# Ordering the graphs' part of a four-layer graph network with the builder's finer engine model

## Chip, core and metric

The kernel runs on one core of a Trainium2 chip. The metric is the device time of one execution in microseconds (us). The engines are TensorE (PE, with its weight loads as PEld), VectorE (DVE), ScalarE (ACT), GpSimd (POOL) and SyncE (SP), which issues the DMAs.

## What is computed

64 graphs of 256 nodes with 128 features pass through four graph layers. Each adds its result to its input and normalizes every node's features:

```
x = layernorm(x + L0(x, adj))   # h[i] = max over j of relu(p[i] + q[j] + b) * adj[i, j]
x = layernorm(x + L1(x, adj))   # elu of three projections, adj @ in, adj^T @ out, tanh(update)
x = layernorm(x + L2(x, adj))   # two GCN steps: norm_A @ (h @ W) + b, elu between
x = layernorm(x + L3(x, adj))   # msg = gelu(layernorm(mj[j] + mi[i] + b1)); agg = sum of msg * adj
...                             # over neighbours; updated = layernorm([x, agg] @ W2 + b2)
```

The adjacency is a matrix of zeros and ones with about 12% ones. L0 and L3 work on every pair of neighbours and make up most of the work.

## The kernel before

Each graph has its 256 nodes in two halves of 128 partitions. The pair layers don't work on all 65,536 pairs: nodes are sorted by their number of neighbours, each node's neighbours are numbered (`rank`), and a table of slots (`RECTS`, 40 slots, 4800 columns per half, `WIDTH`) says how many nodes have at least so many neighbours. A one-hot matrix `hot` (fp8) has one column per pair of slot and node. A matmul with it brings each neighbour's features to that column.

The work of one graph is in four stages, Python generators that `yield` between steps:

- `first` (L502): loads x and adj, transposes adj (matmuls L516, copies `aT` L519), counts and sorts (L528 to L560: VectorE's `kc` L542, ScalarE's four `sign` L551, VectorE's `perm` L560), permutes (L566, L577, copies `nzp` L571, `permT` L581), makes `rank` (L587) and `lack` (L591), writes the table of full slots to memory with eight DMAs (L620), builds `hot` on VectorE in 24 steps (L629, L635), splits the features q into three bf16 parts (`split3`: copy L497, L498 to L500), and takes the maximum over neighbours: per 512 columns three matmuls (L665) and small ones (L681) into a psum piece `bigp`, folded into `lanes` by VectorE (L492; the first piece by ScalarE, L683). It ends with the layernorm.
- `second` (L778, `layer_1` L215): layer 1, with projections (L223, L230), elu (Exp at L194, L200 and L201), aggregation (L238, L240) and update (L249, Tanh L254).
- `third` (L782, `layer_2` L261): the two GCN steps: scaling L293, adjacency matmul L296, copy `agg` L299, weight matmul L304, L308; a double Exp (L194, L198); then the start of layer 3: projections L797, copies L803 and L497, `dT` (L815), and `sums_of` for the first four tiles.
- `last` (L821): the rest of layer 3. It works on ten tiles (five per half: four of 1024 columns and one of 704; tiles 0 to 4 and 5 to 9). `sums_of` (L718) makes a tile's sums with the one-hot matmuls (L728, into `bigp`) and VectorE's additions (L732), squares them (L736), sums the squares (L743, L745) and sends the row to memory (L750). For each pair of tiles it loads the rows back in another layout (`vr`, L762), takes the root and reciprocal (L768: Sqrt L74, reciprocal L75), multiplies by the full slots (L769), and writes the scales to memory (L771). `fetch` (L825) reads them back spread over all partitions (`rs_s`, L828, three buffers). Then a tile is multiplied by its scales (L839), passes Gelu (L841) and is folded into the sums (L492). The end is the aggregation (L860 to L865), the update (L325, L870, L330) and two layernorms, with the output at L336.

`steps` (L881) runs the four stages as a pipeline over the 64 graphs, all unrolled: in step u, `last` works on graph u, `third` on u+1, `second` on u+2, `first` on u+3. `together` (L341) takes the generators' pieces in turn by the share done. This gives the program order, which is only a priority. The builder then orders each engine's instructions itself: it plays the program through a model of the machine, and whenever an engine is free, gives it the ready instruction with the highest priority. Each engine executes the resulting order as it stands. A table load is put before an activation whose function isn't in the table set then loaded; the set of Gelu, that of Exp (with Tanh) and that of Sqrt are needed in turn, while copies, squares and signs stay in the set that is there.

Pools bound how far stages run ahead. `ps_big` (the `bigp` pieces) and `ps_mm` have four psum pieces each, most tiles of `work` and `pair` have one buffer, `hot` has four, `pre` seven.

After the graphs a few instructions test whether a graph broke the table's bounds (`viol`); a general version of the kernel, `general`, is behind a branch and isn't run with these inputs.

Of the kernel before, what the change touches and what calls it, by code (L numbers as in the profile page):

```python
# [43 lines left out]
def kernel(  # L44
# [77 lines left out]
    with tc.tile_pool(name="prep", bufs=1) as prep, tc.tile_pool(  # L122
        name="ps_prep", bufs=2, space=bass.MemoryType.PSUM
# [217 lines left out]
    def together(*gens):  # L341

        gens = [[0, n, gen] for n, gen in gens]
        while gens:
            e = min(gens, key=lambda e: e[0] / e[1])
            e[0] += 1
            if next(e[2], gens) is gens:
                gens.remove(e)
# [5 lines left out]
    def sparse(ctx):  # L354
# [526 lines left out]
        def steps(g0):  # L881
            ss = [{} for _ in range(U)]
            for u in range(1 - len(STAGES), U):
                together(*[
                    (n, part(g0 + u + i, ss[u + i])) for i, (part, n) in enumerate(STAGES) if 0 <= u + i < U
                ])

        if U == B:
            steps(0)
        else:  # L890
            with tc.For_i(0, B, U) as g0:
                steps(g0)
# [201 lines left out]
    with ExitStack() as path:  # L1094
        sparse(path)

    with tc.tile_pool(name="flag", bufs=1) as fp, tc.tile_pool(
        name="ps_flag", bufs=1, space=bass.MemoryType.PSUM
# [44 lines left out]
```

## Time and profile before

| | |
|---|---|
| time, three runs | 5727.94 us median (5721.77 to 5736.96) |
| profiled execution | 5731.62 us, of which the span from first to last instruction 5729.7 us |
| mean granted TensorE clock | 0.862 of full speed |
| busy: DVE, PE, ACT | 4834.4, 4529.9, 4275.2 us |
| ACT table loads on the trace | 1,283 ns each, before L841, L74, L194, L198 and a few others |
| DMA | 365 MB, mean 64 GB/s |
| span per graph in steady state | 87.4 us (174.80 us for two) |

The page gives each engine's busy time and its share of the span, then the chain of work that ended last, followed back from the last instruction, and the groups of instructions by line with their count, busy time, mean duration and the idle time of the engine before them with what ended it. A timeline gives start and duration of each instruction, and in brackets the idle time before it and its releaser. A busy TensorE counts modelled ends of pipelined matmuls. The durations used for the sums are those of this one execution.

### The profile page before, as it was taken

To read this page: it belongs to the slowest core of one execution; us is meant where nothing else is said; L and a number is where in the kernel's file an instruction comes from. 1 tells how busy PE (TensorE), PEld (TensorE's weight loads), DVE (VectorE), ACT (ScalarE), POOL (GpSimd) and SP (SyncE) were. 2 spreads that over 40 slices of the span, in tenths; PEclk is the share of its full clock that TensorE was granted. 3 is DMA by queue.
4 is the path that set the end of the run, shared out by engine and by line. 5 is a ranking of instruction groups with operands and counts; after the bars stand their busy time and mean duration, and the time that the engine had idled before them with its cause. 6 is when DMAs were issued, how large, how long until landed. Compare 5 with 4: busy or idle time off the path is not lost.

```text
span 5729.7 us, 83531 instructions
## 1 busy us (share of the span) xinstructions
PE 4529.9 (79%) x27408; PEld 2508.7 (44%) x27408; DVE 4834.4 (84%) x14654; ACT 4275.2 (75%) x6485; POOL 1.9 (0%) x10
## 2 busy tenths in 40 slices
PE   5878878878778778788788788787887887877875
PEld 2444444444444444444444444444444444444443
DVE  6788888888888888888888888888888888888876
ACT  2577777777777777777777777777777777777785
POOL 0000000000000000000000000000000000000000
PEclk8888889889889889888898898898888887888986
DMA  0122222222212221221221222122212212221222
GB/s 22 44 70 63 62 63 72 62 63 66 69 57 70 65 63 63 72 63 62 63 72 62 63 65 70 59 68 65 63 62 72 64 62 63 69 66 60 68 65 74
DMA packets 292813, 365.15 MB, mean 64 GB/s; under 512 B 151952, under 2 KB 210448, under 8 KB 292368
## 3 DMA queue, kind: packets, MB, share of 16 engines
q1 hardware_dynamic: 292368, 359.73, 20.0%
q8 instruction: 217, 3.56, 0.3%
q14 instruction: 228, 1.87, 0.1%
HBM read 345.07 MB, written 14.53 MB: 63 GB/s over the span
## 4 chain that ended last, share of the span: by engine, by line
PE 52%; DVE 29%; ACT 11%; issue 4%; DMA 3%; SPq 0%; DVEq 0%; POOL 0%; ACTq 0%
PE bigp L665 11%; PE bigp L728 8%; DVE pre L839 6%; PE mm L860 5%; DVE lanes L492 4%; PE mm L743 4%; DVE hot L629 4%; DVE pre L732 4%; DVE sums L492 3%; PE bigp L681 3%; DMA rs_s<-scale_line 2%; PE mm L870 2%; PE mm L296 2%; PE mm L699 2%; PE mm L647 2%
## 5 line engine op out<-in xcount | busy, mean ns | idle before, releaser
L665 PE MATMUL bigp<-hot,q 128*128 128x512 fp8e4 (+1 forms) x3840 | 1052.3, 371 | 66.6 <-DVE lanes L492 52.6
L728 PE MATMUL bigp<-hot,c 128*128 128x512 fp8e4 (+1 forms) x3840 | 928.8, 372 | 140.2 <-DVE pre L732 140.2
L732 DVE TENSOR_TENSOR pre<-bigp,dT 128x512 f32<-128x512 f32 (+6 forms) x1664 | 846.3, 530 | 37.8 <-PE bigp L728 33.5
L492 DVE TENSOR_TENSOR lanes<-bigp,lanes 128x512 f32<-128x512 f32 (+6 forms) x1536 | 772.7, 503 | 94.6 <-PE bigp L681 86.9
L839 DVE TENSOR_TENSOR pre<-pre,rs_s 128x1024 f32<-128x1024 f32 (+1 forms) x640 | 732.9, 1150 | 48.6 <-DMA rs_s<-scale_line 48.0
L736 ACT ACTIVATE sq<-pre 128x1024 f32<-128x1024 f32 (+1 forms) x640 | 638.5, 998 | 169.9 <-DVE pre L732 163.9
L841 ACT ACT_TABLE_LOAD x535 | 686.4, 1283 | 9.5
L492 DVE TENSOR_TENSOR sums<-pre,sums 128x1024 f32<-128x1024 f32 (+6 forms) x1024 | 628.8, 614 | 41.2 <-ACT pre L841 40.7
L745 ACT ACTIVATE row<-mm,eps_t 128x256 f32<-128x256 f32 (+1 forms) x640 | 289.6, 453 | 476.9 <-PE mm L743 476.7
L841 ACT ACTIVATE pre<-pre,be,g 128x1024 f32<-128x1024 f32 (+1 forms) x512 | 594.2, 1172 | 57.8 <-DVE pre L839 53.0
L743 PE MATMUL mm<-sq,ones 128*32 128x256 f32 (+1 forms) x5120 | 482.9, 440 | 135.2 <-ACT sq L736 135.2
L74 ACT ACT_TABLE_LOAD x445 | 570.9, 1283 | 7.5
L728 PEld LDWEIGHTS <-c 128*128 128x128 bf16 x3840 | 331.2, 98 | 550.5 <-issue 136.1
L665 PEld LDWEIGHTS <-q 128*128 128x128 bf16 x3840 | 310.8, 97 | 392.6 <-issue 112.0
L296 PE MATMUL mm<-aT,hs 128*128 128x256 f32 x512 | 232.3, 600 | 316.1 <-DVE hs L293 214.8
L629 DVE TENSOR_SCALAR hot<-rank 128x512 fp8e4<-128x512 bf16 (+5 forms) x1536 | 440.5, 348 | 0.0
L681 PEld LDWEIGHTS <-pick 42*128 42x128 bf16 x2944 | 155.8, 95 | 481.5 <-issue 474.2
L296 PEld LDWEIGHTS mm<-aT,hs 128*128 128x128 f32 x512 | 135.6, 293 | 425.8 <-issue 316.1
L860 PE MATMUL mm<-w3u,sums 128*128 128x128 f32 x2048 | 296.7, 289 | 18.4 <-DVE sums L492 16.1
L194 ACT ACT_TABLE_LOAD x221 | 283.5, 1283 | 3.9
L681 PE MATMUL bigp<-lack,pick 42*128 42x36 bf16 (+16 forms) x2944 | 285.7, 187 | 0.0
L860 PEld LDWEIGHTS mm<-w3u,sums 128*128 128x128 f32 x2048 | 254.5, 195 | 37.3 <-issue 17.6
(226 smaller groups left out, 7132.6 us busy)
## 6 DMA issues: line engine op xcount, KB each, us to landing
rs_s<-scale_line SPq DMA_DIRECT2D x512, 512.0 KB
rs_s<-scale_line SPq DMA_DIRECT2D x128, 352.0 KB
an<-in_adj SPq DMA_DIRECT2D x64, 256.0 KB
x<-in_x SPq DMA_DIRECT2D x64, 128.0 KB
line<-row SPq DMA_DIRECT2D x512, 4.0 KB
out<-o SPq DMA_DIRECT2D x64, 128.0 KB
fu<-fulls SPq DMA_DIRECT2D x192, 4.0 KB
vr<-line SPq DMA_DIRECT2D x192, 8.0 KB
```

Of the source, the lines that this page charges most:

```text
L74: nc.scalar.activation(t, t, AF.Sqrt)
L492: nc.vector.tensor_tensor(lanes[:, :k, :w], src[:, i:i + k], lanes[:, :k, :w], op)
L629: nc.vector.tensor_scalar(hot[:, :, at:at + w], rank[:, :, :w], s0 + i + 1.0 - FAR, None, ALU.is_equal, saturate=False)
L665: nc.tensor.matmul(pt[:, :tl], q3[:, i, h], hot[:, h, t0:t0 + tl], start=i == 0, stop=False)
L681: nc.tensor.matmul(o_, l_, r_, start=False, stop=i == len(todo) - 1)
L728: nc.tensor.matmul(pt[:, :bl], c3[:, k, h], hot[:, h, t0 + b:t0 + b + bl], start=k == 0, stop=k == 2)
L732: nc.vector.tensor_add(block(pre[:, b:], n, w, at), block(pt, n, w, at), widen(dT[:, h, :w], n))
L736: nc.scalar.activation(sq[:, :tl], pre[:, :tl], AF.Square)
L743: nc.tensor.matmul(pr[q * Q:(q + 1) * Q, :tl // 4], ones[:, :Q], v4[:, :, q], start=True, stop=True)
L839: nc.vector.tensor_mul(pre[:, :tl], pre[:, :tl], rs[:, :tl])
L841: nc.scalar.activation(msg[:, :tl], pre[:, :tl], AF.Gelu, bias=be3, scale=g3)
L860: nc.tensor.matmul(pt[:, cols], lanes[:, k, cols], w3u[:, 1], start=k == 0, stop=False)
```

## The change

The call that emits all graphs is put into a named block of its own, and that block is ordered with another machine model of the builder, the one with a finer picture of the engines. The instructions, tiles, pools and program order are the same. Table loads aren't instructions of the kernel; they are put in after the ordering, so their number follows from the order. The block adds a branch on each engine at its start and at its end.

```diff
         if U == B:
-            steps(0)
+            with tc.block(name="graphs", schedule_with_timeline_sim=True):
+                steps(0)
         else:
             with tc.For_i(0, B, U) as g0:
                 steps(g0)
```

In the built programs TensorE, VectorE and ScalarE have the same instructions apart from branches, semaphore waits and table loads. The program before has 1236 table loads in the part that is run, the one after 824, one of them ahead of the block.

## The prediction, made before the changed kernel was run

> **What bounds the kernel now.** I read the page's engine sums first, then the chain that ended last, the costliest groups, and at last a stretch of exactly two graphs (2649.0 to 2823.8 us) engine by engine.
>
> ```profile
> PE 4529.9 (79%) x27408; PEld 2508.7 (44%) x27408; DVE 4834.4 (84%) x14654; ACT 4275.2 (75%) x6485; POOL 1.9 (0%) x10
> PE 52%; DVE 29%; ACT 11%; issue 4%; DMA 3%; SPq 0%; DVEq 0%; POOL 0%; ACTq 0%
> L841 ACT ACT_TABLE_LOAD x535 | 686.4, 1283 | 9.5
> L74 ACT ACT_TABLE_LOAD x445 | 570.9, 1283 | 7.5
> L194 ACT ACT_TABLE_LOAD x221 | 283.5, 1283 | 3.9
> ```
>
> No engine is full. VectorE is nearest, idle (5729.7 - 4834.4)/64 = 14.0 us per graph with the ends of the program. ScalarE spends over 1,500 us on changing tables. The stretch of two graphs, columns as engines with busy us:
>
> ```profile
> 2649.00:2823.80 174.80, 140.39 (x859) 77.58 (x858) 151.88 (x458) 135.85 (x207) 0.00 (x0) 0.89 0.21 67
> ```
>
> A graph takes 87.4 us, and VectorE is idle for (174.8 - 151.88)/2 = 11.5 us of it. Its timeline tells where. I cut the period at the layernorm's last step (L180, end 2652.1) and at the second GCN scaling (L293, end 2680.7). The "head", 28.7 us with 5.7 us idle, builds the one-hot matrix and walks the GCN's short dependent steps. The "rest", 58.4 us with 5.5 us idle, is the dense part. Two waits carry the argument, the first in ScalarE's timeline, the second in VectorE's and SyncE's:
>
> ```profile
> 2667.42 1.28 ACT L198 ACT_TABLE_LOAD   x1
> 2668.72 0.51 ACT L198 ACTIVATE elu_e<-elu_e,minus 128x256 f32<-128x256 f32 x1
> 2669.13 1.04 ACT L736 ACTIVATE sq<-pre 128x1024 f32<-128x1024 f32 x1
> 2670.19 1.28 ACT L841 ACT_TABLE_LOAD   x1
> ```
> ```profile
> 2676.97 0.17 DVE L769 TENSOR_TENSOR vr<-vr,fu 108x16 f32<-108x16 f32 x1
> ...
> 2682.12 0.89 DVE L839 TENSOR_TENSOR pre<-pre,rs_s 128x704 f32<-128x704 f32 x1 [0.53 <-DMA rs_s<-scale_line]
> ```
> ```profile
> 2677.28 0.40 SPq L771 DMA_DIRECT2D scale_line<-vr  x1
> 2677.73 0.36 SPq L764 DMA_DIRECT2D fu<-fulls  x1
> 2678.74 0.35 SPq L828 DMA_DIRECT2D rs_s<-scale_line  x1
> ```
>
> In the head ScalarE is packed and pays a table load before almost every Exp, Gelu or Sqrt. From the last step on a row of scales (L769) to its use (L839) the data goes out to memory and comes back: 0.03 to 0.3 us to the write's issue, 1.46 us to the read's, 3.4 us to the use, 5.0 us in all. For a 1024-wide tile the read takes 3.7 us where L839 waited for it: 5.2 us. Here 4.2 us of VectorE work on average stand between; the wait left is 0.5 us.
>
> **What the Trainium skill says.** "ScalarE: Activation LUTs", What ACT_TABLE_LOAD costs: 1283 ns a load and 1380 ns of drain. The trace agrees on 1283, but the next activation starts 0.01 to 0.02 us after the load's end; I take 1283 alone. "DMA: Bandwidth & Descriptors", Anatomy of one DMA: some 2 us fixed per transfer, mostly the receipt of the last byte. The two transfers here take 1.46 and 3.4 to 3.7 us, near that; the trace's are used. "Perfetto Trace Analysis", Tensor Engine Instruction: ScalarE and VectorE execute strictly in order. The trace agrees: VectorE stands 2.84 us at L226 for a matmul, with independent work behind it. So a misplaced instruction costs its whole wait.
>
> **The change, part by part.** I compared the orders of the two built programs engine by engine, laying the durations of this trace on each queue.
>
> *Removed.* Table loads fall from 1236 to 824: before L841 535 to 313, L74 445 to 378, L194 221 to 129, L198 32 to 1. 412 x 1.283 = 529 us of ScalarE work, 8.3 us per graph. No other work changes: VectorE has 75.1 us per graph both ways, TensorE nearly the same sequence. Loads count only where VectorE or TensorE wait for what lies behind them, so the gain must be followed through the head.
>
> *The head.* From the end of the adjacency's transposed copies (L519): in the new order two Gelus, one load, a row and a square come first (6.0 us), four signs (1.9), load and Exp (1.7); L560's permutations end at 9.4, L197 and the second Exp, now without a load, at 10.4; permT, nzp, permT 1.5, the Exp of io 0.6, rank 0.5: one-hot starts at 13.1 (before: 12.6). L200, L201 and L293 now stand ahead of it, so the first GCN matmul (L296) starts at 13.1 behind L599, not 18.2. One-hot and what lies between take 7.3; L308, load, Exp, L200 and L293 end at 23.5 (before: 27.1). From L180 it is 24.8 instead of 28.7 us. But only 19.6 instead of 22.2 us of VectorE work lie in it; 2.6 us have moved to the rest. Idle in the head: 5.2 instead of 5.7. The visible gain of 3.9 us is 0.5 us net.
>
> *The rest, and a new wait.* The rest has 55.5 instead of 52.8 us of VectorE work. The order puts L839 much closer to L769. VectorE work between them, mean over 48 graphs, before and after: tile 0 7.5 and 4.3 us, tile 2 4.5 and 2.8, tile 4 4.2 and 2.0, tile 8 5.5 and 2.4. The round trip is 5.0 to 5.2. Tile 4: 5.0 - 2.0 = 3.0, less 0.2 for another short wait inside: 2.8 us. Tile 8: 5.2 - 2.4 = 2.8 us, 0.9 of which L498 waits anyway for ScalarE's c. Tile 2's 2.4 us fall into the head, where VectorE would wait for the Gelus: nothing more, and 1 us if that cover goes. Tile 0: covered by the wait for L870. Behind L839 of tile 4 stand the splitting of q (L498 to L500), without which L665 can't go on, so TensorE waits too.
>
> *SyncE's queue.* The fetch of vr for the third group (L762) stands behind the write of the second's scales (L771), and ScalarE's Sqrt, then the copy q, behind it: q is ready at about 31 where tile 4 is released at 33; covered. The eight writes L620 (3.4 us) stand ahead of that L771, whose vr is ready later anyway.
>
> *Other waits of the rest.* Before: 5.5 - 0.5 (tile 4) - 0.6 (L498) = 4.4 us (psum pieces L492 and L732, L330, Sqrt). These depend on how evenly the two big matmul streams are interleaved with their readers; the trace doesn't show the new order. Fewer loads and the stalls above give TensorE and ScalarE time to run ahead: 1.5 us at best. Following the queues piece by piece, with part_max 1.0, L732 2.5, L492 0.4, L330 0.6 and a Gelu behind Sqrt's load 1.3, gives 5.8 at worst. I take 3.0.
>
> *Block.* It adds a branch per engine at each end. The graphs could not start before the preparation's end in the old order either (their first load waits 18.7 us for L440): 0 to 5 us, taken as 0.
>
> *Sum of VectorE's idle time per graph:* 5.2 + 2.8 + 2.8 + 3.0 = 13.8 us against 11.5: +2.3 us, times 64 = +147 us. Profiled execution 5731.6 (span 5729.7), within 0.1% of the median 5727.94: 5728 + 147 = 5875 us.
>
> **Rivals.**
> 1. Faster: ScalarE's loads decide. For it: it is packed in the head, and 11% of the chain is its own. If the head comes out 1.5 us shorter than my sum, tile 8's stall is half hidden (1.5) and the other waits fall to 1.5: 3.7 + 2.8 + 1.5 + 1.5 = 9.5, -2.0 us, 5600 us. It decides where the four terms fall below 11.5. Against it: VectorE, not ScalarE, has least room in the rest, and tile 4's distance is 2.0 us in every one of the 48 graphs.
> 2. No change: the new DMA waits replace the old waits on TensorE one for one (5.2 + 2.8 + 1.9 + 1.6 = 11.5): 5728. That nothing is reordered is excluded; loads and order differ.
> 3. Much slower: other waits at 5.8 us and no cover: 16.6, +5.1 us, 6055 us. For it: strict queues, four psum pieces shared by two streams. Against it: each stall lets the other engines catch up.
>
> **Chances and range.** Forecast 0.54, rival 1 0.21, rival 2 0.10, rival 3 0.15. The measurement can tell about 0.3% (17 us). Faster 0.20, same 0.10, slower 0.70. The range takes most of rivals 1 and 3: 5640 to 6010; the slower cases alone 5760 to 6010.
>
> **What would show it.** Right: table loads near 824 and ScalarE near 3,750 us busy; VectorE still 4,834; idle before L839 on the DMA rs_s from 48 to some 250 to 400 us, tiles 4 and 8 foremost; L296 earlier after L519; q's split late behind tile 4. Wrong: DMA waits under 100 us (then the 5 us round trip is covered by waits I didn't see), or the head shorter by more idle than 0.5 us.

## The result, and the profile after

The changed kernel takes 6335.16 us (median of 4 runs, 6321.98 to 6342.91), the kernel before 5725.73 us beside it: ratio 1.106, 95% interval 1.103 to 1.108, 609 us or 9.5 us per graph slower. The direction was forecast, the size (147 us) was not, and the time lies above the range that was given (5640 to 6010).

The page of the changed kernel: engine sums, the chain that ended last, and five of the costliest groups (count, busy us, mean ns, then the idle time before them and what ended it).

```profile
PE 4742.7 (75%) x27408; PEld 2596.6 (41%) x27408; DVE 4954.8 (78%) x14654; ACT 3794.5 (60%) x6073; POOL 1.9 (0%) x10
DVE 31%; PE 29%; DMA 18%; ACT 17%; issue 4%; SPq 0%; ACTq 0%; POOL 0%; DVEq 0%
L839 DVE TENSOR_TENSOR pre<-pre,rs_s 128x1024 f32<-128x1024 f32 (+1 forms) x640 | 738.2, 1156 | 494.0 <-DMA rs_s<-scale_line 491.8
L841 ACT ACT_TABLE_LOAD x313 | 401.6, 1283 | 5.6
L74 ACT ACT_TABLE_LOAD x378 | 485.0, 1283 | 13.7 <-DMA vr<-line 7.2
```

ScalarE has lost its table loads as forecast (busy 4275 to 3794 us), and the time still rose. In the chain that ended last ScalarE went from 11% to 17% and DMA from 3% to 18%: fewer table loads didn't make a shorter chain. The sum that matters is VectorE's. Its idle time, summed in the trace over the gaps before its instructions, grew from 889 to 1380 us, and its busy time from 4834 to 4955 us: 490 and 120 us, together the whole loss. The list of waits, VectorE's own, of the changed kernel (us in total, times, longest us), and then of the kernel before:

```profile
DVE pre L839 <- DMA rs_s<-scale_line: 491.8, 242, 5.4
DVE vr L75 <- ACT vr L74: 271.2, 178, 5.2
DVE sums L492 <- ACT pre L841: 174.7, 126, 2.3
DVE y L330 <- PE mm L870: 45.2, 58, 9.3
```
```profile
DVE io L226 <- PE mm L223: 179.7, 64, 3.1
DVE rest L498 <- ACT q L497: 93.4, 54, 3.4
...
DVE y L330 <- PE mm L870: 72.1, 64, 4.9
DVE fl L604 <- PE mm L599: 51.0, 64, 2.7
...
DVE pre L839 <- DMA rs_s<-scale_line: 48.0, 57, 4.2
DVE sums L492 <- ACT pre L841: 40.7, 67, 2.3
```

The new order does repair what the old one had: the gap before L226 falls to 15 us, before L498 (on q) to 2.5, before L604 to 5. In their place stand the three longest waits, 938 us together (before: 48 us at L839, 29 at L75 and 41 at L492). The first two are at the end of trips through memory. The timeline of the changed kernel, VectorE and then SyncE's queue, shows one of the 242:

```profile
2928.47 0.17 DVE L769 TENSOR_TENSOR vr<-vr,fu 128x16 f32<-128x16 f32 x1
...
2931.13 0.60 DVE L180 TENSOR_SCALAR x<-y,mv,rs 128x128 f32<-128x128 f32 x2
2934.70 2.46 DVE L839 TENSOR_TENSOR pre<-pre,rs_s 128x1024 f32<-128x1024 f32 x2 [2.97 <-DMA rs_s<-scale_line]
```
```profile
2928.66 0.33 SPq L771 DMA_DIRECT2D scale_line<-vr  x1
...
2930.08 0.84 SPq L828 DMA_DIRECT2D rs_s<-scale_line  x2
```

L769 ends at 2928.64. The write is issued at once, the read at 2930.08, and L839 starts at 2934.70: 6.1 us, of which VectorE has work for three. The second wait has the same shape one trip earlier. ScalarE, then VectorE:

```profile
2905.97 0.47 ACT L745 ACTIVATE row<-mm,eps_t 128x256 f32<-128x256 f32 x1 [3.17 <-PE mm L743]
2908.54 0.37 ACT L865 COPY ak<-mm 128x256 f32<-128x256 f32 x1 [2.10 <-PE mm L862]
2909.69 0.22 ACT L74 ACTIVATE vr<-vr 128x16 f32<-128x16 f32 x1 [0.77 <-DMA vr<-line]
```
```profile
2909.93 0.25 DVE L75 RECIPROCAL vr<-vr 128x16 f32<-128x16 f32 x1 [3.50 <-ACT vr L74]
```

The row of sums is ready at 2906.44, goes out and comes back, and the square root runs at 2909.69. ScalarE stands idle for most of this, so no table load is to blame here; VectorE has already arrived at L75 and waits 3.5 us.

### The profile page after: what moved, and what is told of

It reads as the page before. It is cut to its first block, busy times and chain, and to the rows that moved or that the text cites. A ratio compares the mean times of both kernels' runs of the same rounds, so it can differ in the third digit from the quotient of the medians.

```text
span 6340.9 us, 83074 instructions
## 1 busy us (share of the span) xinstructions
PE 4742.7 (75%) x27408; PEld 2596.6 (41%) x27408; DVE 4954.8 (78%) x14654; ACT 3794.5 (60%) x6073; POOL 1.9 (0%) x10
## 4 chain that ended last, share of the span: by engine, by line
DVE 31%; PE 29%; DMA 18%; ACT 17%; issue 4%; SPq 0%; ACTq 0%; POOL 0%; DVEq 0%
DMA rs_s<-scale_line 11%; PE bigp L665 8%; DVE pre L839 6%; DVE hot L629 6%; PE bigp L728 6%; DMA scale_line<-vr 4%; DVE pre L732 4%; DVE sums L492 3%; PE mm L860 3%; ACT pre L841 3%; PE mm L743 2%; PE mm L810 2%; ACT sign L551 2%; ACT sq L736 2%; DVE lanes L492 2%
## 5 line engine op out<-in xcount | busy, mean ns | idle before, releaser
L665 PE MATMUL bigp<-hot,q 128*128 128x512 fp8e4 (+1 forms) x3840 | 1068.0, 381 | 230.3 <-DVE lanes L492 104.7
L839 DVE TENSOR_TENSOR pre<-pre,rs_s 128x1024 f32<-128x1024 f32 (+1 forms) x640 | 738.2, 1156 | 494.0 <-DMA rs_s<-scale_line 491.8
L732 DVE TENSOR_TENSOR pre<-bigp,dT 128x512 f32<-128x512 f32 (+6 forms) x1664 | 836.1, 531 | 13.1 <-PE bigp L728 10.3
L492 DVE TENSOR_TENSOR lanes<-bigp,lanes 128x512 f32<-128x512 f32 (+6 forms) x1536 | 780.6, 508 | 76.6 <-PE bigp L681 41.9
L492 DVE TENSOR_TENSOR sums<-pre,sums 128x1024 f32<-128x1024 f32 (+6 forms) x1024 | 635.5, 621 | 181.1 <-ACT pre L841 174.7
L207 PE MATMUL mm<-ident,x 128*128 128x128 f32 x512 | 163.5, 419 | 540.6 <-DVE x L180 540.6
L728 PEld LDWEIGHTS <-c 128*128 128x128 bf16 x3840 | 349.5, 100 | 397.1 <-issue 119.0
L296 PE MATMUL mm<-aT,hs 128*128 128x256 f32 x512 | 269.3, 654 | 318.7 <-DVE hs L293 318.7
L743 PE MATMUL mm<-sq,ones 128*32 128x256 f32 (+1 forms) x5120 | 466.5, 437 | 47.0 <-ACT sq L736 46.3
L207 PEld LDWEIGHTS mm<-ident,x 128*128 128x128 f32 x512 | 80.7, 200 | 607.6 <-DVE x L180 572.4
L296 PEld LDWEIGHTS mm<-aT,hs 128*128 128x128 f32 x512 | 148.6, 321 | 423.9 <-issue 342.2
L75 DVE RECIPROCAL vr<-vr 128x16 f32<-128x16 f32 (+1 forms) x320 | 79.1, 247 | 271.5 <-ACT vr L74 271.2
```

The source lines that it names most:

```text
L296: nc.tensor.matmul(pa[:, :N], hs[:, h], aT[:, h], start=h == 0, stop=h == H - 1)
L492: nc.vector.tensor_tensor(lanes[:, :k, :w], src[:, i:i + k], lanes[:, :k, :w], op)
L665: nc.tensor.matmul(pt[:, :tl], q3[:, i, h], hot[:, h, t0:t0 + tl], start=i == 0, stop=False)
L728: nc.tensor.matmul(pt[:, :bl], c3[:, k, h], hot[:, h, t0 + b:t0 + b + bl], start=k == 0, stop=k == 2)
L732: nc.vector.tensor_add(block(pre[:, b:], n, w, at), block(pt, n, w, at), widen(dT[:, h, :w], n))
L743: nc.tensor.matmul(pr[q * Q:(q + 1) * Q, :tl // 4], ones[:, :Q], v4[:, :, q], start=True, stop=True)
```

## The experiments

Three theories went in. A: the new order puts the consumers of two trips through memory (rows to L74 and L75, scales to L839) too close behind their producers. B: it does so everywhere, so that what is taken away at one place comes back at the next. C: ScalarE's order makes its results late; a variant, L, says because of table loads that the order knows nothing of. Line numbers in these kernels are shifted by the lines added above.

**The block alone.**

```diff
-            with tc.block(name="graphs", schedule_with_timeline_sim=True):
+            with tc.block(name="graphs"):
```

> The graphs in a block of their own, ordered with the same model as before. Theory (the finer model's order costs the time): 5726 +- 17 us, as before. Rival (the block's boundary costs): near 6335 us.

5730.82 us, ratio 1.000 (0.999 to 1.001). So the block's boundary costs nothing that can be measured, and the order is all of it.

**One trip cut, the order left free.** L839's scales come from a constant row in memory.

```diff
-                    nc.sync.dma_start(rs[:, :TODO[i][2]], s.pop(("scale", i)).broadcast_to([P, TODO[i][2]]))
+                    nc.sync.dma_start(rs[:, :TODO[i][2]], flat[:, :TODO[i][2]].broadcast_to([P, TODO[i][2]]))
```

> Old model; the spread scales rs_s are read from a constant row in memory instead of the row that L771 has written, so L839 waits for no round trip from L769 (the transfers stay, the scales are all ones). Theory (round trips through memory behind in-order queues): little lost here before, so little gained: L839's 49 us and what follows from it, 5620 to 5720 us.

> The finer model, with the same constant row for the scales. Theory (round trips): the 492 us at L839 go, the waits at L75 for the rows' round trip stay, 5750 to 6000 us, that is at most 300 us over the old model with the same cut. Rival (the interleaving itself: dependent VectorE instructions stand side by side, and Gelu and Sqrt are bunched): 6200 us or more.

With the builder's other model 5688.13 us, ratio 0.993 (0.991 to 0.994), as expected. With the finer one 6508.93 us, ratio 1.136 (1.134 to 1.138): the wait for the scales is gone and the kernel is 174 us slower than with it, in the range of the rival (the interleaving itself). The finer model had made yet another order, with 1379 table loads.

**Both trips cut, the order left free.**

```diff
-            nc.sync.dma_start(vr[:rows], line[:, :n].rearrange("o (p k) -> (o p) k", k=PIECE))
+            nc.sync.dma_start(vr[:rows], flat[:, :n].rearrange("o (p k) -> (o p) k", k=PIECE))
```

> The finer model, with constants read back at both round trips: the rows' (vr, L762) and the scales' (rs_s, L828); all transfers stay, the row sums and scales that were computed are not used. Theory (round trips): no wait on a DMA of this chain is left, and fewer table loads show: 5450 to 5700 us. Rival (the interleaving itself): 6100 us or more.

6345.73 us, ratio 1.107 (1.105 to 1.109). Theory A missed by 646 us, though only 831 table loads were left; the time again lies in the rival's range. The waits of VectorE in this kernel:

```profile
DVE vr L76 <- ACT vr L75: 313.9, 165, 4.3
DVE pre L736 <- PE bigp L732: 205.8, 155, 5.1
DVE kc L546 <- PE mm L538: 173.5, 63, 2.8
DVE pre L843 <- ACT sq L740: 169.7, 118, 4.5
```

L843 is L839: it now waits 170 us, with its data long there, because it stands behind a square of ScalarE that must read `pre` first. These two runs with the finer model test that model more than the theory, since each edit gives a new order. From here on orders are held: each engine's instructions are chained in a listed order, with edges that carry no semaphore. In the traces of these kernels TensorE, VectorE and ScalarE go through the graphs in just that order.

```diff
...
+for seq in _pinned().values():
+    for a, b in zip(seq, seq[1:]):
+        tc.add_manual_dep(
+            made[first_at + b], made[first_at + a].name,
+            mybir.DependencyInfo(mybir.DependencyClass.NoSync, mybir.DependencyReason.DATA),
+            reason="pinned",
+        )
```

**Both trips cut, orders held.** The cut of the last kernel, first with the order of the changed kernel, then with that of the kernel before.

> The order of every engine's instructions is held at exactly that of the changed kernel (824 table loads); the two reads from memory (the row scales rs_s ahead of L839, and the scores of a group of four tiles turned into vr ahead of L74) come from a constant row that was written at the start, so that neither waits for a write. The scales are then all ones and the scores constant; the arithmetic is the same in count. Theory A (the order is bad because it places the consumers of two trips through memory too close behind their producers): the 492 us at L839 and most of the 271 us at L75 go, and not more than 150 us of it comes back elsewhere: 5650 to 5850. Theory B (the order leaves so little slack everywhere that the next producer is late when one wait is taken away): most of it comes back, 6050 to 6300. Theory C (ScalarE's order: results come late whatever memory does): above 6150, with the waits on ScalarE at L75 and L492 as large as before.

> The same cut with the order of every engine held at that of the kernel before (1236 table loads): the yardstick for cut_both_same_order. The kernel before idles 48.6 us at L839 on the read of rs_s and 29 us at L75: 5640 to 5720 by every theory. The difference between the two then says what the new order costs or brings when no trip through memory is waited for: about zero by theory A, 350 to 600 by theories B and C.

6186.69 us, ratio 1.080 (1.078 to 1.083), and 5729.23 us, ratio 1.000 (0.9995 to 1.001). The yardstick lies 9 us above its range: its wait at L839 fell only from 48 to 19 us, and its time didn't fall. Holding the order and this cut together cost nothing (VectorE is idle for 890 us with both and for 889 without); no run holds an order and changes nothing else. The cut was too weak for a verdict, though the first kernel lies in the ranges of theories B and C: this wait of it is left, on a read that needs no write.

```profile
DVE pre L863 <- DMA rs_s<-flat: 358.4, 253, 4.4
```

The read stands behind the write of scale_line in SyncE's queue, and that write waits for L769. Only the write's own 1.5 us were cut.

**One engine kept in its old order.** The finer model orders the block around VectorE's old order, then around ScalarE's.

> The finer model orders the block, but VectorE's instructions are held in the order of the kernel before; the model is left to order ScalarE, TensorE and SyncE around that (1238 table loads, so the order of ScalarE comes out near the old one too). Theories A and B put the cost into VectorE's order: 5700 to 5800, with L839 under 80 us on the read of rs_s. Theory C puts it into ScalarE's and the others': 5900 or more, with VectorE waiting for ScalarE.

> The finer model orders the block, but ScalarE's instructions are held in the order of the kernel before (1236 table loads); VectorE's order is the model's, built around that. Theory A: the model still places L839 right behind the tile's scale_line: over 300 us at L839, 6000 to 6300. Theory B: 6000 to 6300 with the waits at other places. Theory C: 5700 to 5800.

6445.55 us, ratio 1.125 (1.123 to 1.127), and 7137.76 us, ratio 1.247 (1.245 to 1.249). With VectorE's order untouched the loss is greater, 717 us. A and B missed that by 645 us; C had the time but not the waits, since the largest of them are for TensorE's results (L330, L604 and L226, 700 us together). The second lies outside every theory's range. So the cost is not a property of one engine's order.

**Both trips taken off the path altogether.** All DMAs are issued, but into a tile that nobody reads, or into an `rs_s` that nobody reads; the square root and L839 take a constant tile. The pool of `rs_s` gives up one buffer for it.

```diff
-            nc.sync.dma_start(vr[:rows], line[:, :n].rearrange("o (p k) -> (o p) k", k=PIECE))
+            nc.sync.dma_start(unread[:rows, :PIECE], line[:, :n].rearrange("o (p k) -> (o p) k", k=PIECE))
...
-            inverse_root(vr[:rows])
+            nc.scalar.activation(vr[:rows], level[:rows, :PIECE], AF.Sqrt)
+            nc.vector.reciprocal(vr[:rows], vr[:rows])
...
-                    nc.vector.tensor_mul(pre[:, :tl], pre[:, :tl], rs[:, :tl])
+                    nc.vector.tensor_mul(pre[:, :tl], pre[:, :tl], level[:, :tl])
```

> Every engine's order held at exactly that of the changed kernel, as in cut_both_same_order, and the cut made deeper: all DMAs are still issued, but the read of the row scores lands in a tile that nobody reads, L74's square root takes a constant tile instead, and L839 multiplies by that constant tile and not by rs_s. So no instruction of VectorE or ScalarE waits for a trip through memory at all, and SyncE's queue holds up neither. The scales are then constant; the arithmetic is the same in count. In cut_both_same_order 359 us of waiting at L839 were left, because the read stands behind the write of scale_line in SyncE's queue. Theory A (trips through memory): 5700 to 5850. Theory B (no slack anywhere in the order): 5950 to 6150, as the 359 us come back in part at L75, at the sum tree L492 and on TensorE's results. Theory C (ScalarE's results come late): above 6050, with L75 and L492 as in the changed kernel or above.

6070.64 us, ratio 1.061 (1.059 to 1.063): theory B's range, and C's too by the time alone. The 492 us of waiting at L839 are gone, those at L75 fell from 271 to 184, and the time fell by 265. Where the rest came back (L515 is L492, L792 the reciprocal of L75):

```profile
DVE sums L515 <- ACT pre L865: 325.6, 243, 3.3
DVE vr L792 <- ACT vr L791: 184.0, 132, 2.6
```

The sum tree's wait for the Gelu grew from 175 to 326 us. The Gelu reads what L839 writes; with L839 earlier, VectorE comes earlier to the sum tree that follows, and waits there.

**One engine alone reordered.** The other three are held in the order of the kernel before. Each of these orders is again a new one, made around the three that are held.

> The finer model may order VectorE alone: TensorE, ScalarE and SyncE are held in the order of the kernel before (1236 table loads). Theory A or B with the cost in VectorE's order: 6000 or more. If the cost is in the way that the four orders work together, or in another engine's order: 5700 to 5800.

> The finer model may order ScalarE alone: VectorE, TensorE and SyncE are held in the order of the kernel before; 1146 table loads, 90 fewer. Theory C (ScalarE's order makes results late): 5900 or more. If ScalarE has room (75 per cent busy before): 5680 to 5750.

> The finer model may order TensorE alone: VectorE, ScalarE and SyncE are held in the order of the kernel before (1236 table loads). fine_model_old_vectore, with VectorE's old order, lost 717 us, and its three largest waits on VectorE were for TensorE's results at the layers' y, fl and io (700 us of 1634 us idle). If TensorE's order causes these: 6000 to 6400. If not: 5680 to 5800.

7157.52 us, ratio 1.250 (1.248 to 1.252); 6116.42 us, ratio 1.069 (1.067 to 1.071); 6089.53 us, ratio 1.063 (1.061 to 1.065). Each lies in the range that puts the cost into that engine's order, so the finer model loses on each of the three, by far the most on VectorE. There the three waits of the changed kernel appear again, 1129 us together against 938:

```profile
DVE pre L858 <- DMA rs_s<-scale_line: 447.1, 255, 5.4
DVE sums L511 <- ACT pre L860: 372.0, 279, 2.3
DVE vr L94 <- ACT vr L93: 309.9, 203, 4.2
```

ScalarE alone, with 90 table loads fewer, loses 392 us, and there VectorE waits for TensorE (L604, L226) and for q.

**Table loads taken away.** With orders held, every Gelu, Exp, Tanh and Sqrt becomes an Identity of the same operands: 824 or 1236 loads become one.

```diff
-        nc.scalar.activation(t, t, AF.Sqrt)
+        nc.scalar.activation(t, t, AF.Identity)
...
-                    nc.scalar.activation(msg[:, :tl], pre[:, :tl], AF.Gelu, bias=be3, scale=g3)
+                    nc.scalar.activation(msg[:, :tl], pre[:, :tl], AF.Identity, bias=be3, scale=g3)
```

> Every engine's order held at exactly that of the changed kernel; every Gelu, Exp, Tanh and Sqrt is computed as Identity instead, with the same operands, so that one table load is left of 824. The outputs' values are others. Theory L (the order supposes that ScalarE delivers without table loads): the waits for ScalarE at L75 (271 us), at L492 (175 us) and at L200 and L75 rs (80 us) go for the most part, those for rs_s partly: 5650 to 5900, no more than 250 us above no_loads_old_order. Theory B (tight for other reasons): 6050 or more, 400 us or more above no_loads_old_order.

> The same replacement with every order held at that of the kernel before (1236 table loads gone): the yardstick. VectorE waited some 270 us for ScalarE in the kernel before; ScalarE loses 1236 x 1.283 = 1586 us of its 4,274: 5500 to 5680 by every theory.

> The order of the changed kernel with both taken away: no table loads, and no instruction of VectorE or ScalarE that waits for a trip through memory (as in deep_cut_same_order). Theory L: the order then meets what it supposes, 5400 to 5600, level with no_loads_old_order or below it. Theory B: 5800 or more.

> no_loads_deep_same_order with every order held at that of the kernel before: no table loads, no instruction of VectorE or ScalarE that waits for a trip through memory. Of no_loads_old_order's 5664 the wait at L839 (84 us) and part of that at L75 (33 us) go: 5560 to 5640. The distance to no_loads_deep_same_order, 5859, is then what neither trips nor loads explain: 220 to 300 us.

| | order of the changed kernel | order of the kernel before | distance |
|---|---|---|---|
| nothing taken away | 6335.16 | 5725.73 | 609 |
| no table loads | 6179.80, ratio 1.080 (1.078 to 1.082) | 5663.92, ratio 0.989 (0.987 to 0.991) | 516 |
| no table loads, no trips | 5858.75, ratio 1.023 (1.022 to 1.025) | 5609.94, ratio 0.980 (0.977 to 0.982) | 249 |

Both yardsticks came as expected, theory L missed both of its kernels and B had them: loads explain 93 of the 609 us. (Without its loads the new order is 155 us faster, the old one 62.) Waits of VectorE without them, in the new order:

```profile
DVE pre L859 <- DMA rs_s<-scale_line: 508.0, 248, 5.4
DVE vr L95 <- ACT vr L94: 260.2, 172, 4.7
DVE sums L512 <- ACT pre L861: 53.5, 52, 1.1
```

The sum tree's wait falls from 175 to 54 us, as L said, but the square root's stays (271 to 260), and so does that of L839 (492 to 508). Taking the trips away as well brings the distance from 516 to 249: 267 us for the trips. The engine sums of the two kernels of the last row, new order and old:

```profile
PE 4629.4 (79%) x27408; PEld 2562.9 (44%) x27408; DVE 4942.7 (84%) x14655; ACT 2690.9 (46%) x5250; POOL 1.9 (0%) x10
```
```profile
PE 4514.5 (81%) x27408; PEld 2508.8 (45%) x27408; DVE 4799.4 (86%) x14655; ACT 2698.4 (48%) x5250; POOL 1.9 (0%) x10
```

143 of the 249 us are VectorE's busy time, for the same instructions; 100 us are idle time (901 against 801 us in the trace). The durations of the instructions add up to nearly the same, 5,877 and 5,858 us, but neighbours overlap by 934 us in all in the one and by 1,058 in the other: 124 of the 143 us. Of the 100 us of idle time 52 are gaps of under 0.15 us, and only 47 are longer waits.

**More distance in program order.** AHEAD is 6; the finer model is free.

```diff
-        AHEAD = 4
+        AHEAD = 6
```

> The finer model orders the block; AHEAD is 6 in place of 4 and the pool of pre holds 9 buffers in place of 7, so that a tile's row sums are asked for two tiles earlier in program order (977 table loads). If distance in program order is what L839 lacks: under 6000, with under 200 us at L839 on rs_s. If the model uses up any distance by placing the other work first: 6200 to 6600.

6707.42 us, ratio 1.171 (1.169 to 1.173), above even the 6200 to 6600 of the less hopeful expectation. The wait at L839 is still 386 us, and 322 us are new at L732 on TensorE. But the kernel that ran has seven buffers for `pre`, as before, and not the nine of the expectation. With six tiles made ahead, a lack of buffers could hold up the next ones, and this run can't tell that from what the model does with the distance. Whether distance in program order is what was lacking stays open.

**VectorE's neighbours made independent.** The maxima of the first layer's fold go alternately into two spare halves and read a constant, instead of reading what the neighbour wrote. For room, L839 takes its constant from a narrower tile, repeated (616.6 us busy in its 1024-wide form, 616.5 without).

```diff
-                    nc.vector.tensor_tensor(lanes[:, :k, :w], src[:, i:i + k], lanes[:, :k, :w], op)
+                    if op == ALU.max:
+                        turn[0] += 1
+                        out = spare[:, turn[0] % 2, :k * w].rearrange("p (s k) -> p s k", s=k)
+                        nc.vector.tensor_tensor(out, src[:, i:i + k], ones[:, :1].unsqueeze(2).broadcast_to([P, k, w]), op)
...
```

> no_loads_deep_same_order, and in the fold of the first layer's lanes (832 of the instructions at L492 read what the one before wrote in some order) each maximum is taken with a constant and written to one of two spare halves in turn, so that none depends on its neighbour; the outputs' values are others, the number and shapes of the instructions the same. If an instruction behind its own producer costs 0.115 us more (0.034 behind the end against 0.081 ahead of it): 516 such gaps among the lanes and 108 ahead of total_m, 60 to 75 us: VectorE busy 4,870 to 4,885, time 5780 to 5805. If the busy time is long for another cause: 5840 to 5870.

5816.55 us, ratio 1.016 (1.013 to 1.019). VectorE's busy time falls by 68 us, within what was expected:

```profile
PE 4593.4 (79%) x27408; PEld 2549.0 (44%) x27408; DVE 4874.6 (84%) x14655; ACT 2691.6 (46%) x5250; POOL 1.9 (0%) x10
```

The time falls by only 42 us, less than expected, since 23 us come back as idle time: gaps of under 0.15 us fall by 32 us, longer waits grow by 55. The mechanism can be read in the changed kernel's timeline:

```profile
2912.40 0.17 DVE L492 TENSOR_TENSOR lanes<-part_max,lanes 128x12 f32<-128x12 f32 x1
2912.61 0.43 DVE L688 TENSOR_TENSOR total_m<-lanes 128x256 f32<-128x256 f32 x1
...
2926.77 0.42 DVE L706 TENSOR_TENSOR m<-mm,m 128x256 f32<-128x256 f32 x1
2927.10 0.68 DVE L732 TENSOR_TENSOR pre<-bigp,dT 128x512 f32<-128x512 f32 x1
```

L688 reads what its neighbour wrote and starts 0.04 us after its end (2912.57). L732 does not, and starts 0.09 us before the end of its neighbour (2927.19). In the new order 2,636 instructions read a tile of the name that their neighbour wrote, 1,270 in the old; a quarter of these overlap against 60%. A name covers several buffers and halves of a tile, so not all of these pairs depend: the two halves of `hs` at L293 overlap in each of 128 pairs, and L492 after L492 on the same `lanes` in none of 683. Starts at 0 to 0.06 us behind the neighbour's end, whatever the names, number 1,641 in the new order and 573 in the old.

No experiment here gave an order that beats the kernel before and computes the same.

## Why the prediction was wrong

What held. Loads fell to 824 and ScalarE's busy time to 3,794 us (3,750 forecast). That the loads lie for the most part off the path was the right reading: taking 1,586 us of them from ScalarE wins 62 us in no_loads_old_order, and the 824 that are left, 1,057 us, win 155 in the new order. The cause named first, L839 too close behind L769, is the largest single wait. But the direction came out as forecast by part of the cause only: tiles 4 and 8 wait 3.7 us per graph, of a loss of 9.5. The step that failed most is the term "other waits of the rest", taken at 3.0 us per graph: the rest is idle for 14.2 us, 10.4 of them outside tiles 4 and 8.

What failed, step by step:

- "Tile 2's 2.4 us fall into the head, where VectorE would wait for the Gelus: nothing more". Tile 2 waits 3.1 us on average, the longest of all, in 63 of 64 graphs. Over 48 graphs, from the last L180 ahead of the one-hot part to L293, the head went from 27.1 to 25.8 us with idle time from 4.8 to 5.9 us (forecast: 5.7 to 5.2 in one graph). The 2.8 us before L226 went, and 3.1 us before L839 came. The head was treated as a stretch with idle time to share, but the new order had removed the longest part of it.
- "Tile 4: ... 2.8 us. Tile 8: ... 2.8 us", tile 0 "covered". Measured 2.2, 1.5 and 0.5 us. The mechanism was right, the sizes of tiles 4 and 8 too high; with tile 2 L839 waits 494 us, forecast 250 to 400.
- "SyncE's queue ... covered". This looked at the fetch of vr as a matter of its place in a queue, and not as what it is, the end of a second trip through memory, with a matmul, a row and a square root in series. It was the same argument as for L839 and was not applied: VectorE's work between the last L732 of a group and L75 fell from 8.4 to 4.0 us in the first group and from 10.7 to 5.3 in the last. L75 waits 271 us against 29, 3.8 us more per graph. The timeline above shows it with ScalarE idle.
- "Other waits of the rest ... I take 3.0" (before: 4.4). Over 48 graphs, idle time of the rest went from 7.4 us per graph (5.5 in the one that was laid out) to 14.2. L75 is in this, and the sum tree's wait for the Gelu alone added 134 us, 2.1 us per graph. The forecast let stalls give the other engines "time to run ahead"; the runs don't show it. In deep_cut_same_order 492 us of waiting at L839 and 87 at L75 are removed and 265 us won, as the next consumer stands close too. Rival 3 pointed this way ("strict queues", "no cover") and priced it at 5.1 us per graph; it is 9.5. Its sum of 16.6 leaves out the 1 us that it says the lost cover would cost.
- "VectorE has 75.1 us per graph both ways". It has the same instructions, but 120 us more busy time, 1.9 us per graph; 89 of the 120 us are overlap of neighbours that is gone. This term was missing: no step asked which instructions become neighbours. The figure was low before, too: the stretch has 151.88/2 = 75.9 us, as the head holds 23.0 us of work (28.7 less 5.7) and not 22.2. With that the head wins 1.3 us and not 0.5, and the forecast would have been about 50 us lower; the slip didn't cause the miss.

The loss comes apart in the table above, in the order in which things were taken away: 93 us table loads, 267 us trips through memory, 249 us neither, of which 143 us are busy time, nearly all of it neighbours that no longer overlap (68 us shown in one loop, the rest argued from the count of neighbours), and 100 us idle time, half of it short gaps between neighbours. The shares overlap: the trips alone with orders held and loads in place give back 265 us of the new order, and the old order wasn't run so.

What stays open is why the finer model makes tight orders on each engine. It may price these instructions otherwise than the chip takes them, but no run here shows it; table loads, which are put in only after the ordering, account for 93 us.

## What to carry to other kernels

An engine's queue that runs strictly in order suffers from an order without slack: sum the work between each producer and its consumer for every trip that leaves the engine, all of them and not the first one found, and compare it with the measured trip. A repaired wait is worth its size only if the next consumer has slack; taking away both trips here (492 and 87 us of waiting) was worth 265 us. To learn what a scheduler's order costs, hold the order and take causes away one at a time, since an edit under a free scheduler gives a new order and answers another question.

## What the runs showed of the hardware

- On VectorE, an instruction that reads what its neighbour wrote starts some 0.034 us after the neighbour's end (median of the pairs by name in the changed kernel), one that doesn't some 0.08 us before it: a difference of some 0.115 us a pair. The changed kernel has 1,068 more of the late starts, by estimate 1,068 x 0.115 = 123 us; the traces have 89 us less overlap and 40 us more of short gaps.
- The trip from L769 through memory to L839 took 5.4 to 6.2 us on average in the tiles that waited most in the new order (tiles 4 and 2), 5.0 to 5.2 in the old. The read alone took 4.7 us at tile 2 and 3.9 at tile 4; in the stretch shown above two more reads (fu and x) and a write (out) are issued within 2 us of tile 2's. Whether that is why wasn't tried.
- The granted TensorE clock fell broadly with the time in these runs: 0.875 at a span of 5607 us, 0.849 at 5852, 0.819 at 6341, 0.782 at 7134, and the same 27,408 matmuls were busy for 4,515, 4,629, 4,743 and 4,888 us. Part of the loss may be this feedback, an engine that waits and then runs slower; it wasn't tried apart.
